# A recurrent layer and a mixture of experts in one kernel: a written order for the token sort, single fetches of the experts' rows, and small moves in the recurrent ticks

## The chip, the cores and the metric

The kernel runs on one core of a Trainium2 chip. A core has five engines that work beside each other and meet by semaphores: TensorE (PE in the profile; its weight loads are PEld), VectorE (DVE), ScalarE (ACT), GpSimd (POOL) and SyncE (SP), and 16 DMA engines. The metric is the device time of one launch in microseconds (us), as the median of several runs. Beside it stands one profiled execution, whose trace gives every instruction its start and duration.

## What is computed

The input is x, two sequences of 1024 tokens of 256 numbers, and one condition vector per sequence. Two layers are added to x, one after the other:

```python
# 1. two GRU layers over time, fed by a mixed input, with a gate from the condition
mixed = tanh(x @ W_in.T + b_in + cond)
h1 = gru(mixed, Wih0, Whh0, ...);  h2 = gru(h1, Wih1, Whh1, ...)
#   step: r = sigmoid(xr + hr); z = sigmoid(xz + hz); n = tanh(xn + r * hn)
#         h = (1 - z) * n + z * h
gate = sigmoid(cond @ W_gate.T + b_gate)
x = x + (gate * h2 + h2) @ W_out.T + b_out

# 2. a shared inner layer (512 wide) and 8 experts (256 wide), two experts a token
shared = (silu(xf @ w1) * (xf @ w3)) @ w2
s = sigmoid(concat(xf, cond) @ router_W);  top 2 of s + router_bias
gates = s[top] / sum(s[top])                      # 1/2 each where the sum is tiny
routed = sum over the two: gates * (gelu(xf @ W1e[e]) @ W2e[e])
x = x + (shared + routed) / 3
```

Everything is float32.

## The kernel before

**The ticks.** Each sequence is cut into 16 chunks, so that 32 chunks (the rows of a step) go through the recurrence at once. A first pass (`AHEAD`) gives each chunk a state to start from. The program is unrolled into 126 ticks; in one tick layer 0 makes a step and layer 1 makes the step that layer 0 had two ticks before. A step is `add_state` (the state times Whh, on TensorE, 16 matmul records) and `finish_scanned`: a sigmoid of two gates on ScalarE, a scan on VectorE, a tanh on ScalarE, a second product and a second scan on VectorE, and a transposition of the new row, which is the next step's weight operand. Each step waits for the one before, and both layers take turns on the same engines. Other work is hung into the ticks by name: `place(tick, where, what)` with `where` one of "product" (on TensorE, behind layer 0's products), "n0" (ScalarE), "scan0" and "scan1" (VectorE, between the tanh and the second scan of layer 0 or 1), "behind" and "end". `front.prepare` returns ten such small things that compute the condition's gate and the gated output weights. All of this stands in `tc.manual_schedule()`, in which each engine issues its instructions in the written order. At position -33 of a layer (ticks 29 and 31) the row that is the sequence's true beginning is set to zero by a mask (`keep_of`, `kept`); at position 0 (ticks 62 and 64) a layer starts its real pass from the state `begin`, whose turned form is `start_row`.

**The hidden parts.** The shared inner layer is computed in 16 parts, one for each block of 512 tokens (`TB`) and each 128 of the 512 inner columns. A part is a w1 sum and a w3 sum on TensorE (two matmuls each, of two records each), a sigmoid on ScalarE (`sig`), and two products on VectorE (`silu`, then the part itself, `front.hid`). Part 0 is computed in the last ticks; the other 15 are the list `parts`. The first `EARLY` of them run beside the sort, the next one behind the experts, and `parts[FILL:]` in the tail.

**The sort.** `moe` finds for each token its two experts, counts tokens by expert, gives each token's copy a slot so that blocks of 128 slots belong to one expert, and makes `pick` (which token sits in a slot) and `words` (which expert owns a block). That is a chain of some 50 VectorE instructions with two products on TensorE in it: a sum over all tokens (`ps_all`, `ps_before`), and `ps_pick`. The gates of the choice (`mine`, `denom`, `share`) follow it in the text. Here nothing fixes the order: the scheduler mixes the sort, the gates and the hidden parts on each engine.

**The experts.** `go_through` runs over 35 blocks of 128 slots (`SURE`), four more if a count asks for them (the branch). A block is fetched by an indirect DMA that GpSimd issues (`fetch`, L1274), turned on TensorE, multiplied with W1e, passed through gelu, turned, multiplied with W2e, and written to `back` in HBM.

**The tail.** A second written region. `fetch_back` issues an indirect DMA (L1335) that brings the experts' rows of 128 tokens for one of their two choices. Eight are issued at once. Then each part of `parts[FILL:]` is computed, and two more fetches are issued behind it: so that they don't run ahead, a one-element copy on GpSimd (the marker, L1334) reads one of the part's tiles and writes into the fetch's target. Only every second fetch has a marker. `add_gone` adds fetched rows, times their share, to `base` (L1349). Then 16 tiles follow: one more fetch, the product with w2 (`ps_s`, L1367, 8 records), an addition to `base` (L1375), and the output's DMA (L1376). All sums go through the seven PSUM banks of `p_any`, in turn.

Of the kernel before, what the change touches and what calls it, by code (L numbers as in the profile page):

```python
# [70 lines left out]
EARLY = 8  # L71
# [14 lines left out]
def gru_moe(ctx, tc, xT, vec, bias, w_in, wih0, whh0, wih1, whh1, w_out, w_gate, router, w1, w3, w2, w1e, w2e, out):  # L86
# [62 lines left out]
    class Steps:  # L149
# [177 lines left out]
        def finish_scanned(self, layer, to, tick, before_n, after_n, between, keep=None):  # L327
# [7 lines left out]
            if keep is not None:  # L335
                kept = self.edge.tile([P, U], FP, name=f"kept{layer}")
                nc.vector.tensor_scalar(kept, h, keep, -1.0, ALU.mult, ALU.mult)
                h = kept
# [14 lines left out]
            n = self.step_pool.tile([P, U, 2], FP, name=f"n{layer}")  # L353
            before_n()
# [46 lines left out]
    with ExitStack() as stack:  # L401
        g = Steps(stack, "", on_pe=False, rest_of_x=rest_of_x)
        g.gates = [
# [138 lines left out]

        def let_wait(ins, copied):


            if ins is not None and copied is not None:
                sync = mybir.DependencyInfo(mybir.DependencyClass.Sync, mybir.DependencyReason.DATA)
                tc.add_manual_dep(ins.ins, copied.ins.name, sync, reason="the next product adds to it")
# [48 lines left out]
        places = {}  # L597

        def place(tick, where, what):
            places.setdefault((tick, where), []).append(what)  # L600

# [49 lines left out]
        for i, todo in enumerate(front.prepare(g.bank)):  # L651
            for where, what in todo.items():
                place(AHEAD[0] - 8 + i, where, what)
# [32 lines left out]
        with tc.manual_schedule():  # L686
            for tick in range(AHEAD[0] + S + LAG):
                now = [layer for layer in range(2) if runs(layer, tick)]
                for layer in now:
                    if layer not in g.states:  # L690
                        g.states[layer], g.rows[layer] = zero_state, zero_row
                    elif position(layer, tick) == 0:
                        g.starts[layer] = g.states[layer] = begin[layer]
                        g.start_rows[layer] = g.rows[layer] = turned(g.starts[layer], f"start_row{layer}")
# [127 lines left out]
class Front:  # L822
# [17 lines left out]
    def prepare(self, bank):  # L840
# [3 lines left out]
        def gate_sums():  # L844
            ps["gate"] = bank("ps_gate")[:, 0 : KD * B].rearrange("p (k b) -> p k b", b=B)
            for m in range(KD):
                for k in range(KD):
                    last = nc.tensor.matmul(
                        out=ps["gate"][:, m, :],
                        lhsT=later["w_gate"][:, k, m * P : (m + 1) * P],  # L850
                        rhs=vec_sb[:, COND + k * B : COND + (k + 1) * B],
                        start=(k == 0),
                        stop=(k == KD - 1),
                    )
            return last
# [35 lines left out]
        def keep_context():  # L891
# [3 lines left out]
            {"product": gate_sums, "scan1": lambda: spread(0)},  # L895
            {"n0": gates, "scan1": lambda: spread(1)},
# [113 lines left out]
def moe(ctx, tc, tag, front, out):  # L1010
# [67 lines left out]
    def wide(t):  # L1078
        return t.to_broadcast([P, NT, E])

    iota = expert.unsqueeze(1).to_broadcast([P, NT, E])
    raw = rt("raw")
    nc.vector.tensor_tensor(raw, logits[:, :, 0:E], context.unsqueeze(1).to_broadcast([P, NT, E]), ALU.add)
    s = rt("s")
    nc.scalar.activation(s, raw, AF.Sigmoid)
    sel = rt("sel")
    nc.vector.tensor_tensor(sel, s, vec_sb[:, RBIAS : RBIAS + E].unsqueeze(1).to_broadcast([P, NT, E]), ALU.add)
    chosen = []
    for i in range(2):
        top = rt(f"top{i}", NT, 1)  # L1090
        nc.vector.tensor_reduce(top, sel, AX.X, ALU.max)
        at = rt(f"at{i}")
        nc.vector.tensor_tensor(at, sel, wide(top), ALU.is_equal)

        place = rt(f"place{i}")
        nc.vector.scalar_tensor_tensor(place, iota, float(E), at, ALU.subtract, ALU.mult)
        first = rt(f"first{i}", NT, 1)
        nc.vector.tensor_reduce(first, place, AX.X, ALU.min)
        nc.vector.tensor_scalar(first, first, float(E), None, ALU.add)
        one = rt(f"one{i}")  # L1100
        nc.vector.tensor_tensor(one, iota, wide(first), ALU.is_equal)
        chosen.append(one)
        if i == 0:
            rest = rt("rest")
            nc.vector.scalar_tensor_tensor(rest, one, -BIG, sel, ALU.mult, ALU.add)
            sel = rest
    both = rt("both", dtype=BF)
    nc.vector.tensor_tensor(both, chosen[0], chosen[1], ALU.add)


    for to, which in ((ps_all.rearrange("p (e t) -> p e t", e=E), every), (ps_before, before)):
        nc.tensor.matmul(out=to, lhsT=which, rhs=both.rearrange("p t e -> p e t"), start=True, stop=True)
    upto = rt("upto", E, NT)
    nc.vector.tensor_tensor_scan(
        upto.rearrange("p e t -> p (e t)"), running.rearrange("p e t -> p (e t)"), ps_all, 0.0, ALU.mult, ALU.add
    )

    whole = rt("whole", E, dtype=I32)
    nc.vector.tensor_scalar(whole, upto[:, :, NT - 1], float(P - 1), None, ALU.add)
    nc.vector.tensor_scalar(whole, whole, -P, None, ALU.bitwise_and)  # L1120
    size = rt("size", E)
    nc.vector.tensor_copy(size, whole)
    end = rt("end", E)
    nc.vector.tensor_tensor_scan(end, adding, size, 0.0, ALU.mult, ALU.add)
    slots_taken = rt("slots_taken", 1, dtype=I32)
    nc.vector.tensor_copy(slots_taken, end[:, E - 1 : E])
    start = rt("start", E)
    nc.vector.tensor_tensor(start, end, size, ALU.subtract)

    slot = rt("slot", E, NT)  # L1130
    nc.vector.tensor_tensor(slot, upto, ps_all.rearrange("p (e t) -> p e t", e=E), ALU.subtract)
    nc.vector.tensor_tensor(slot, slot, ps_before, ALU.add)
    nc.vector.tensor_tensor(slot, slot, start.unsqueeze(2).to_broadcast([P, E, NT]), ALU.add)
    slot_of = rt("slot_of", 2, NT)
    for c in range(2):
        own = rt(f"own{c}")
        nc.vector.tensor_tensor(own, chosen[c], slot.rearrange("p e t -> p t e"), ALU.mult)
        nc.vector.tensor_reduce(slot_of[:, c, :].unsqueeze(2), own, AX.X, ALU.add)
    slots = rt("slots", 2, NT, dtype=I32)
    nc.vector.tensor_copy(slots, slot_of)  # L1140
    block = rt("block", 2, NT, dtype=I32)
    nc.vector.tensor_scalar(block, slots, -P, None, ALU.bitwise_and)
    high = rt("high", 2, NT)
    nc.vector.tensor_copy(high, block)
    low = rt("low", 2, NT)
    nc.vector.tensor_tensor(low, slot_of, high, ALU.subtract)

    in_block = rt("in_block", 2, NT, NB, dtype=F16)
    at_lane = rt("at_lane", 2, NT, P, dtype=F16)
    for c in range(2):  # L1150
        nc.vector.tensor_tensor(
            in_block[:, c, :, :],
            block_start.unsqueeze(1).to_broadcast([P, NT, NB]),
            high[:, c, :].unsqueeze(2).to_broadcast([P, NT, NB]),
            ALU.is_equal,
        )
        nc.vector.tensor_tensor(
            in_block[:, c, :, :],
            in_block[:, c, :, :],
            token.unsqueeze(2).to_broadcast([P, NT, NB]),  # L1160
            ALU.mult,
        )
        nc.vector.tensor_tensor(
            at_lane[:, c, :, :],
            lane.unsqueeze(1).to_broadcast([P, NT, P]),
            low[:, c, :].unsqueeze(2).to_broadcast([P, NT, P]),
            ALU.is_equal,
        )
    for c in range(2):
        for t in range(NT):  # L1170
            nc.tensor.matmul(
                out=ps_pick,
                lhsT=at_lane[:, c, t, :],
                rhs=in_block[:, c, t, :],
                start=(c == 0 and t == 0),
                stop=(c == 1 and t == NT - 1),
            )
    pick = rt("pick", NB, dtype=I32)
    nc.vector.tensor_scalar(pick, ps_pick, float(N - 1), None, ALU.min)

    past = rt("past", NB, E)
    nc.vector.tensor_tensor(
        past,
        block_start.unsqueeze(2).to_broadcast([P, NB, E]),
        end.unsqueeze(1).to_broadcast([P, NB, E]),
        ALU.is_ge,
    )
    nc.vector.tensor_reduce(owner.rearrange("p w i -> p (w i)")[:, 0:NB].unsqueeze(2), past, AX.X, ALU.add)
    shifted = rt("shifted", NW, IDS)
    nc.vector.scalar_tensor_tensor(  # L1190
        shifted, owner, float(E - 1), power.unsqueeze(1).to_broadcast([P, NW, IDS]), ALU.min, ALU.mult
    )
    word = rt("word", NW, 1)
    nc.vector.tensor_reduce(word, shifted, AX.X, ALU.add)
    words = rt("words", NW, dtype=I32)
# [255 lines left out]
```

## Time and profile before

| | us |
|---|---|
| runs | 535.58, 538.12, 537.25 |
| median | 537.25 |
| the profiled execution | 538.56 |
| its span | 536.8 |
| busy in it: PE, PEld | 512.1, 341.2 |
| busy in it: DVE, ACT, POOL | 385.1, 243.6, 76.9 |

| stretch of the span | what runs |
|---|---|
| 0 to 10 | loads, first mixed input |
| 10 to 360 | the ticks |
| 360 to 389 | last group's output, the sort, hidden parts |
| 389 to 476 | the experts |
| 476 to 537 | the tail |

How to read it: times in the timeline are from the span's start; a row gives start, duration, engine, line, operation, output<-inputs and shapes, and in brackets how long the engine idled before and what ended that. A float32 matmul has two records. A matmul's start is recorded, its end is modelled.

### The profile page before, as it was taken

Reading aid. Unit: us, or ns where it says so; the run is one execution under the profiler, and the core shown is the slowest. Engines: PE = TensorE matmul, PEld = TensorE weight load, DVE = VectorE, ACT = ScalarE, POOL = GpSimd, SP = SyncE. Lnnn points to the kernel's source line nnn. Section 1 sums busy time; section 2 is a strip of 40 time slices with the busy share of each in tenths; the row PEclk is TensorE's granted clock in tenths of the full one; section 3 lists DMA queues with packets and bytes.
Section 4 is the critical chain, followed back from the end, with each engine's and each line's share of the span. In section 5 each row is a group of like instructions: output and inputs, shape, how many; then the busy total and the mean of one; then the engine's idle time right before and its main releaser. Section 6 shows DMA issues by size and latency. Waiting matters only on the chain. (4 is left out here: it accounts for less than half of the span.)

```text
span 536.8 us, 18511 instructions
## 1 busy us (share of the span) xinstructions
PE 512.1 (95%) x7492; PEld 341.2 (64%) x7492; DVE 385.1 (72%) x1296; ACT 243.6 (45%) x833; POOL 76.9 (14%) x124
## 2 busy tenths in 40 slices
PE   7999999999999999999999999989999999999795
PEld 4556766666665545665665666654458888854584
DVE  3665789999888888888888888888953333336372
ACT  3444355655665656656666565641133333341000
POOL 1200000000000000000000000002064444037570
PEclk9999999999999999999999999999999999999888
DMA  8980000000000000000000000001024443223252
GB/s 283 373 259 2 2 3 4 3 4 2 4 32 3 12 1 4 2 23 22 3 23 2 23 22 4 22 21 61 1 88 128 120 125 123 70 72 104 81 177 85
DMA packets 23103, 32.13 MB, mean 60 GB/s; under 512 B 3056, under 2 KB 18544, under 8 KB 22992
## 3 DMA queue, kind: packets, MB, share of 16 engines
q1 hardware_dynamic: 17344, 19.94, 11.0%
q0 software_dynamic: 3216, 8.79, 5.8%
q10 hardware_dynamic: 2448, 2.11, 1.2%
q8 instruction: 63, 1.03, 0.8%
q14 instruction: 32, 0.26, 0.2%
HBM read 21.26 MB, written 9.57 MB: 57 GB/s over the span
## 5 line engine op out<-in xcount | busy, mean ns | idle before, releaser
L296 PE MATMUL ps_step<-whh_sb,h 128*32 128x192 f32 x3616 | 193.3, 331 | 5.4 <-DVE h L369 4.2
L296 PEld LDWEIGHTS ps_step<-whh_sb,h 128*32 128x32 f32 x3616 | 94.6, 109 | 71.4 <-DVE h L369 51.9
L360 DVE TENSOR_TENSOR_SCAN row<-gates,n 128x128 f32<-128x128 f32 x230 | 98.0, 426 | 29.6 <-ACT n L355 28.3
L344 DVE TENSOR_TENSOR_SCAN ps_step<-gates,ps_step 128x128 f32<-128x128 f32 x230 | 97.3, 423 | 15.0 <-ACT gates L341 15.0
L268 PE MATMUL ps_step<-wih_sb,h 128*32 128x192 f32 x1696 | 99.7, 328 | 4.1 <-ACT ps_step L526 2.4
L355 ACT ACTIVATE n<-ps_step 128x64 f32<-128x64 f32 x228 | 53.0, 232 | 111.0 <-DVE ps_step L344 110.9
L341 ACT ACTIVATE gates<-ps_step 128x128 f32<-128x128 f32 x230 | 66.5, 289 | 35.5 <-PE ps_step L296 26.0
L268 PEld LDWEIGHTS ps_step<-wih_sb,h 128*32 128x32 f32 x1696 | 57.4, 110 | 26.8 <-ACT ps_step L526 14.5
L369 DVE STREAM_TRANSPOSE h<-row 128x64 f32<-128x64 f32 x230 | 56.5, 246 | 8.0
L969 PE MATMUL ps_w<-x_sb,w_sb 128*128 128x512 f32 x128 | 57.3, 597 | 0.2 <-PEq L1320 0.2
L268 PE MATMUL ps_in<-wih_sb,h 128*32 128x192 f32 x1024 | 54.4, 328 | 1.8 <-ACT h L257 1.4
L1239 DVE COPY hT<-ps_hT 128x256 f32<-128x256 f32 x35 | 14.9, 425 | 49.0 <-PE ps_hT L1237 47.1
L526 ACT COPY ps_step<-inputs 128x256 f32<-128x256 f32 x123 | 47.8, 389 | 0.0
L357 DVE SCALAR_TENSOR_TENSOR n<-gates,row 128x64 f32<-128x64 f32 x224 | 47.0, 210 | 0.0
L268 PEld LDWEIGHTS ps_in<-wih_sb,h 128*32 128x32 f32 x1024 | 34.0, 110 | 14.6 <-issue 4.6
L526 ACT COPY ps_step<-bt 128x256 f32<-128x256 f32 x106 | 39.9, 376 | 3.3
L1274 POOL DMA_INDIRECT inputs<-given,pick x35 | 33.3, 951 | 55.2 <-PE ps_xT L1237 31.9
L969 PEld LDWEIGHTS ps_w<-x_sb,w_sb 128*128 128x128 f32 x128 | 23.6, 190 | 27.1 <-issue 24.7
L1245 PE MATMUL ps_h<-w1e_sb,xT 128*128 x140 | 36.1, 380 | 0.7 <-DVE xT L1239 0.7
L1245 PE MATMUL ps_y<-w2e_sb,hT 128*128 x140 | 36.0, 380 | 0.0
L1335 POOL DMA_INDIRECT inputs<-back,slots x32 | 30.9, 964 | 30.0 <-issue 28.3
L1245 PEld LDWEIGHTS ps_y<-w2e_sb,hT 128*128 128x128 f32 x140 | 26.4, 190 | 4.8 <-DVE hT L1239 1.3
(179 smaller groups left out, 430.9 us busy)
## 6 DMA issues: line engine op xcount, KB each, us to landing
back<-y SPq DMA_DIRECT2D x35, 128.0 KB
w1e_sb<-in_w1e SPq DMA_DIRECT2D x1, 2048.0 KB
w2e_sb<-in_w2e SPq DMA_DIRECT2D x1, 2048.0 KB
given<-inputs SPq DMA_DIRECT2D x8, 256.0 KB
out_dram<-inputs ACTq DMA_DIRECT2D x16, 128.0 KB
whh_sb<-in_whh SPq DMA_DIRECT2D x2, 768.0 KB
x_sb<-in_xT SPq DMA_DIRECT2D x3, 512.0 KB
w_sb<-in_w SPq DMA_DIRECT2D x3, 512.0 KB
```

The source lines that it names most:

```text
L268: last = nc.tensor.matmul(out=out[cols(q), :, :], lhsT=given(k), rhs=self.wih[layer][:, k, q * 3 * U : (q + 1) * 3 * U].rearrange("p (g u) ...
L296: nc.tensor.matmul(out=by_sum(self.sums[layer])[cols(q), 0:3, :], lhsT=self.states[layer][:, k, :], rhs=self.whh[layer][:, k, q * 3 * U : ...
L341: nc.scalar.activation(gates[:, :, :, 1], sums[:, 1:3, :], AF.Sigmoid)
L344: nc.vector.tensor_tensor_scan(s, gates[:, 0, :, :].rearrange("p u i -> p (u i)"), ps[:, 0 : 6 * U : 3], 0.0, ALU.mult, ALU.add,)
L355: nc.scalar.activation(n[:, :, 0], s[:, 1 : 2 * U : 2], AF.Tanh, scale=-1.0 if keep is None else keep)
L357: nc.vector.scalar_tensor_tensor(n[:, :, 1], gates[:, 1, :, 1], 1.0, h, ALU.subtract, ALU.mult)
L360: nc.vector.tensor_tensor_scan(row.rearrange("p u i -> p (u i)"), gates[:, 1, :, :].rearrange("p u i -> p (u i)"), n.rearrange("p u i -> p ...
L369: nc.vector.transpose(to, row)
L526: return nc.scalar.copy(by_sum(banks[layer][tick % 2])[:, 0:4, :], g.sum_bias[1] if layer else inputs[:, group_of(0, tick), :, :],)
L969: last = self.tc.nc.tensor.matmul(out=ps, lhsT=self.later[name][:, k, m * P : (m + 1) * P], rhs=self.x1[:, k, blk * TB : (blk + 1) * TB], ...
L1245: nc.tensor.matmul(out=ps, lhsT=of[:, k, :], rhs=weights_sb[:, bass.ds(e * KD + k, 1), :], start=(k == 0), stop=(k == KD - 1),)
L1274: nc.gpsimd.indirect_dma_start(out=xg, out_offset=None, in_=given[:, :], in_offset=bass.IndirectOffsetOnAxis(ap=pick[:, i : i + 1], axis=0),)
```

## The change

- *Ticks.* The mask leaves `finish_scanned`; it is made by `mask(layer)`, placed one step earlier ("scan1" of tick 28 for layer 0, "scan0" of tick 31 for layer 1). The turned start row is made behind the first scan of its step and not ahead of the step. `gate_sums` is cut in two, one half a tick earlier, so `prepare` begins a tick earlier.
- *Sort.* It stands in a `manual_schedule` region, with six hidden parts at written places. In these parts ScalarE also copies the w3 sum out of PSUM (`look`), VectorE makes only the first product, and GpSimd makes the second (`silu_of`).
- *Gates last.* `mine` to `share` move from behind the sort to behind the experts, ahead of the branch.
- *`EARLY` is 7*, so one hidden part more (seven) lies in the tail.
- *Single fetches.* Each fetch in the tail whose caller gives a tile has a marker.

```diff
-EARLY = 8
+EARLY = 7
...
-            if keep is not None:
-                kept = self.edge.tile([P, U], FP, name=f"kept{layer}")
-                nc.vector.tensor_scalar(kept, h, keep, -1.0, ALU.mult, ALU.mult)
-                h = kept
...
+            if h is self.turned_row.get(layer):
+                nc.vector.transpose(h, self.states[layer])
             before_n()
...
+        def mask(layer):
+            kept = edge.tile([P, U], FP, name=f"kept{layer}")
+            nc.vector.tensor_scalar(kept, g.rows[layer], not_first[:, 0:1], -1.0, ALU.mult, ALU.mult)
+            g.rows[layer] = kept
+        place(AHEAD[0] - FIRST - 2, "scan1", lambda: mask(0))
+        place(AHEAD[0] + LAG - FIRST - 1, "scan0", lambda: mask(1))
...
-                place(AHEAD[0] - 8 + i, where, what)
+                place(AHEAD[0] - 9 + i, where, what)
...
-                        g.start_rows[layer] = g.rows[layer] = turned(g.starts[layer], f"start_row{layer}")
+                        g.start_rows[layer] = g.rows[layer] = g.turned_row[layer] = edge.tile(
+                            [P, U], FP, name=f"start_row{layer}"
+                        )
...
-            {"product": gate_sums, "scan1": lambda: spread(0)},
-            {"n0": gates, "scan1": lambda: spread(1)},
+            {"product": lambda: gate_sums(0), "scan1": lambda: spread(0)},
+            {"product": lambda: gate_sums(1), "scan1": lambda: spread(1)},
+            {"n0": gates},
...
+    def look(i):
+        factors[i] = [wk.tile([P, TB], FP, name=name) for name in ("sig", "silu", "other")]
+        nc.scalar.activation(factors[i][0], begun[i, "w1"], AF.Sigmoid)
+        nc.scalar.copy(factors[i][2], begun[i, "w3"])
+
+    def silu_of(i):
+        (blk, m), (sig, silu, other) = parts[i], factors[i]
+        nc.vector.tensor_tensor(silu, begun[i, "w1"], sig, ALU.mult)
+        nc.gpsimd.tensor_tensor(front.hid(m, slice(blk * TB, (blk + 1) * TB)), silu, other, ALU.mult)
+
+    with tc.manual_schedule():
+        sums_of(0)
...            # the sort, as before, with these calls in it:
+                look(0); sums_of(1); silu_of(0)          # behind the first choice's rest
...
+        look(1); sums_of(2)                              # behind the two counting matmuls
...
+        silu_of(1)                                       # behind slot
...
+        look(2); sums_of(3)                              # behind low
...                                                      # in_block[c], at_lane[c], then:
+            silu_of(2 + c)
+            if c == 0:
+                look(3); sums_of(4)
+        sums_of(5, ("w1",), [0])
...            # 32 matmuls for ps_pick, pick
+        look(4); silu_of(4); sums_of(5, ("w1",), [1]); sums_of(5, ("w3",))
...            # past, owner, shifted, word, words
+        look(5); silu_of(5)
+    shared_hidden(parts[6:EARLY])
...
     front.hidden(blk, m, *sums, *(wk.tile([P, TB], FP, name=name) for name in ("sig", "silu")))
+    mine = rt("mine", 2, NT)
...            # the gates' lines, moved here unchanged
...
-        if behind is not None and i % 2 == 0:
+        if behind is not None:
             nc.gpsimd.tensor_copy(yb[0:1, 0:1], behind[0:1, 0:1])
```

(Calls that stand on lines of their own in the kernel are joined by semicolons here.)

## The prediction

> **What bounds the kernel now.** I read the page's slices first, then the chain that ended last, then the timeline in three places: the ticks, the sorting (365 to 397 us) and the tail (476 us on). All times below are those of the one profiled execution (538.56 us; its span of 536.8 leaves 1.8 outside); the median of the runs is 537.25, so I take 1.3 off at the end.
>
> ```profile
> PE   7999999999999999999999999989999999999795
> PEclk9999999999999999999999999999999999999888
> ```
>
> TensorE is busy everywhere, but up to about 360 us that is a loop of short steps (a tick is 2.74 us, from one start of layer 0's gates to the next) in which TensorE, VectorE and ScalarE hand over to each other. From 365 us on it is plain TensorE work: whatever moves there moves the end only by TensorE's idle time and by its clock. The chain says the same of the tail, and shows a hole:
>
> ```profile
> 476.11 20.84 PE ps_w L969 x48
> 496.95 6.26 PE ps_s L1367 x29
> 503.21 0.46 issue
> ...
> 504.75 1.05 issue
> ...
> 506.26 1.65 issue
> 507.90 23.23 PE ps_s L1367 x94
> ```
>
> ```profile
> 496.00:503.00 7.00, 7.00 (x32) 5.65 (x31) 0.69 (x1) 0.60 (x1) 5.14 (x8) 1.00 0.33 94
> 503.00:508.00 5.00, 1.84 (x7) 1.28 (x7) 2.45 (x5) 0.00 (x0) 2.91 (x3) 0.87 0.37 107
> 508.00:513.50 5.50, 5.50 (x14) 4.12 (x14) 4.71 (x12) 0.00 (x0) 2.48 (x4) 0.50 0.28 91
> 513.50:531.20 17.70, 17.62 (x82) 15.18 (x80) 9.91 (x25) 0.00 (x0) 8.52 (x12) 1.00 0.53 160
> ```
>
> (The windows view: length, then busy time of PE, PEld, DVE, ACT and POOL; clock; DMA share; GB/s.) TensorE stops for 3.16 us between 503 and 508, and then runs at clock 0.50. The tail's price: 48 rows of w1/w3 at 0.43 and 128 rows of the w2 products at 0.216 (an undisturbed tile of 8 rows takes 1.73) are 20.6 + 27.6 = 48.2 us; from 476.11 to the last row's end at 531.1 it took 55.0. So 6.8 us are lost there. Just before, results of TensorE are taken late:
>
> ```profile
> 500.23 0.60 ACT L981 ACTIVATE sig<-ps_w 128x512 f32<-128x512 f32 x1 [6.71 <-PE ps_s L1367]
> 503.70 0.69 DVE L983 TENSOR_TENSOR inputs<-silu,ps_w 128x512 f32<-128x512 f32 x1 [2.15 <-remote]
> 508.65 0.42 DVE L1375 SCALAR_TENSOR_TENSOR inputs<-ps_s,inputs 128x256 f32<-128x256 f32 x1 [2.43 <-remote]
> ```
>
> The last inner part's w1 sum was due near 495.3, its sigmoid starts at 500.2; the first w2 tile was due near 498.7, its addition starts at 508.65. No row tells why; seven banks full of untaken sums fit TensorE's stop.
>
> The sorting's rows:
>
> ```profile
> 373.10 0.39 PE L1112 MATMUL few<-both,every 128*128 128x128 bf16 x1 [0.70 <-DVE both L1108]
> 388.06 0.19 DVE L1179 TENSOR_SCALAR pick<-few 128x39 int32<-128x39 f32 x1
> 388.55 1.18 POOL L1274 DMA_INDIRECT inputs<-given,pick  x1 [19.99 <-DVE pick L1179]
> 396.70 1.13 PE L1245 MATMUL ps_h<-w1e_sb,xT 128*128 x4 [0.68 <-DVE xT L1239]
> ```
>
> VectorE works without a break from 374 to 389, yet TensorE idles only 0.70 + 0.12 + 0.68 = 1.5 us here, for eight inner parts of 8 x 0.43 = 3.44 us fill it.
>
> **The change, part by part.** *The ticks.* Ticks 29, 31, 54 and 64 are 0.20, 0.19, 0.40 and 0.49 longer than 2.74.
>
> ```profile
> 92.12 0.21 DVE L337 TENSOR_SCALAR kept<-row,not_first 128x64 f32<-128x64 f32 x1
> 160.83 1.05 PE L848 MATMUL ps_gate<-vec_sb,w_gate_sb 128*128 128x2 f32 x8
> 189.77 0.24 DVE L484 STREAM_TRANSPOSE start_row<-begin 128x64 f32<-128x64 f32 x1
> ```
>
> The mask stands ahead of the scan that the tick waits for; moved one step up into the 0.18 us in which VectorE waits for the tanh, it saves about 0.1 each (the tanh with a scale tensor, 0.33 against 0.23, stays). Half of the gate sums, 0.53, fits a tick's slack, since ticks with a whole input piece (0.83) last 2.74 too: the 0.40 goes. The turned start row moves behind the scan, beside the tanh, and saves 0 to 0.2 (the rest of tick 64's excess is the go-round's copies, which stay). Sum -0.7 (-0.9 to -0.3, all on the path).
>
> *The sorting.* Out of VectorE's queue ahead of pick go some 2.5 us of gates, 1.5 us of block owners, and the second products (0.68 each); four first products (0.60 each in a row of independent steps) stay. But dependent steps follow each other at 0.32 where independent ones take 0.20, and the written order has nothing between them. Step by step: `both` at 371.4, earlier than TensorE ends its second part (365.27 + 2 x 3.44 = 372.15), so the two counting matmuls start there, not at 373.10, and the 0.70 hole closes. From the scan (372.85) to in_block took 5.7, now about 4.9: 377.75. Two rounds of 0.72 + 0.85 + 2.2 and one product of 0.6: 385.9. Pick at about 386.9, 1.2 us earlier than 388.06.
> TensorE meanwhile: 372.6 + three parts + a quarter part = 383.8, 16 pick matmuls (0.5), then nothing allowed until 386.0: **a hole of 1.6 us** (2.4 if GpSimd beside it slows VectorE by a tenth). Then 0.55 + 2.6 + 3.44: the filling ends at 392.6.
> The first fetch now stands behind GpSimd's products. A 128x512 product on GpSimd is not in the trace; bounds are VectorE's 0.69 and twice GpSimd's one-input row (128x512, 1.50), I take 1.5, being nearest that row in engine and size. Product 3 ends at 388.0, so fetch 0 starts no later than before; whether products 4 and 5 come between the fetches is the scheduler's. If not, TensorE's wait at the first expert stays 0.68; if both do, fetches 0 and 1 start near 391 and 393.5 and it is about 3.0. I take 1.7. Sum: 1.6 + 1.7 - 1.5 = **+1.8** (-0.8 if neither hole opens, +3.9 with both at their worst).
> [...]
> ScalarE's six copies (0.6 each, as its sigmoid of that size) hide: it is busy 15% of the time there. The gates' steps (2.5 us) move behind the experts, where VectorE is a third busy and the first share is wanted at 483.86; uncovered they would cost 2.5.
>
> *One part moved to the tail, single fetches.* The part's 3.44 us only changes place. GpSimd now issues a marker (0.18, with 0.27 behind it) before each of 23 fetches (11 before): 9 x 1.25 + 23 x 1.42 = 43.9 us, under a TensorE tail of 51.7; before it was 42.2 under 48.2. So fetches gain 1.6 us of room and cost nothing. Behind each marker wait all later fetches, and VectorE's first product of part k+2 now waits for the marker that reads part k's; by these periods the last starts at 500.4 on the old axis, with its bank wanted six tiles later. What the 6.8 us become is the open term: 0 to 6.8 back. I take 6.6, since all three late rows sit where the last part meets the w2 tiles, and that meeting is moved and re-spaced.
>
> **The rivals.** *A, the stop in the tail goes:* 538.56 - 0.7 + 1.8 - 6.6 = 533.1, less 1.3: **531.8** (529.5 to 535.5 with the terms' bounds). For it: the run of tiles after 513.5 keeps clock 1.00 with the same gathers and output writes. Against: its cause is not in the rows.
> *B, the stop stays:* what held TensorE's results was not the pairing of fetches. 538.56 - 0.7 + 1.8 - 1.3 = **538.4** (536 to 540.5). For it: fetches still follow each other within 1.4 us, and the runs of before lie within 2.5 us, so they all seem to pay.
> *C, slower: the stop stays and the hole ahead of pick halves the clock.* In the tail the clock went to 0.50 after 3.16 us of stops in about 5. The same 6.8 us at half clock cost 3.4: B + 3.4 = **541.8** (540 to 545). It decides once a hole, with what lies beside it, leaves TensorE idle for more than about 2 us of 3.4; at 360.10 an idle 1.29 us did not do it. My holes are 1.6 to 3.0.
> [...]
>
> **How the numbers follow.** A 0.43, B 0.30, C 0.27. A tenth of A falls within the 0.5% (2.7 us, about what measurement can tell from no change), a tenth of B beyond it as faster, a little as slower; C is nearly all slower. Faster 0.42, same 0.30, slower 0.28. The range runs from A's lower part to C's upper middle, 530 to 541.5; A alone is 529.5 to 535.5.
>
> **What would show it.** Right: no PE "issue" rows in the chain between parts and w2 tiles, and clock 1.00 to the end; ticks 29, 31, 54 near 2.8; pick near 387 on the old axis with PE idle about 1.6 ahead of it; DMA_INDIRECT for pick waiting on GpSimd's product, not on pick. Wrong: clock 0.50 in the sorting (C), a stop of 3 us again among the w2 tiles (B), or TensorE idle over 4 us ahead of the first expert.

## The result, and the profile after

The changed kernel takes **541.21 us** (median of seven runs, 540.17 to 543.61); the kernel before takes 537.59 on the same chip (seven runs, 535.58 to 538.83). The ratio is 1.0066, 95% interval 1.0042 to 1.0089: slower by 0.7%, where the likeliest case of the forecast (A, 531.8) was faster. The profiled execution took 540.17 us with a span of 538.4 (before: 538.56 and 536.8).

The page's slices after (TensorE's busy tenths and its granted clock):

```profile
PE   8999999999999999999999999989698999999995
PEclk9999999999999999999999999999999999999998
```

The dip in the tail at slice 38 is gone; the 6 at slice 29, at 377 to 390 us, is new. The chain that ended last (start, length, what):

```profile
479.27 24.27 PE ps_w L982 x56
503.54 8.52 PE ps_s L1421 x39
512.06 0.33 issue
...
513.49 0.33 issue
...
514.28 0.23 issue
514.51 18.30 PE ps_s L1421 x84
```

From the tail's start to the last w2 row it is 53.5 us for 51.7 of work, with three short stops and at full clock. Before it was 55.0 for 48.2. So the tail lost 1.8 us instead of 6.8: **5.0 less**. The windows of the sorting (length; busy time of PE, PEld, DVE, ACT and POOL; clock; DMA share; GB/s) show where more than that went:

```profile
384.60:388.90 4.30, 0.04 (x2) 0.03 (x2) 4.26 (x4) 0.80 (x2) 1.33 (x1) 1.00 0.01 2
388.90:392.40 3.50, 3.50 (x20) 1.95 (x21) 3.24 (x6) 0.60 (x1) 2.63 (x3) 0.51 0.02 5
```

TensorE stands still for 4.3 us while VectorE is busy throughout, and then runs 3.4 us at half clock. The timeline tells what VectorE did until then:

```profile
369.16 0.28 DVE L1355 TENSOR_TENSOR score<-one,s 128x128 f32<-128x128 f32 x1
369.20 1.37 POOL L1122 TENSOR_TENSOR h<-silu,other 128x512 f32<-128x512 f32 x1 [1.44 <-DVE silu L1121]
369.36 1.36 DVE L1138 TENSOR_TENSOR at<-rest,top 128x128 f32<-128x128 f32 x1
...
373.95 0.41 DVE L1164 TENSOR_TENSOR_SCAN upto<-running,few 128x128 f32<-128x128 f32 x1
...
377.04 1.29 POOL L1122 TENSOR_TENSOR inputs<-silu,other 128x512 f32<-128x512 f32 x1 [6.47 <-issue]
377.42 1.13 DVE L1188 TENSOR_TENSOR own<-one,slot 128x128 f32<-128x128 f32 x1
380.51 0.81 DVE L1210 TENSOR_TENSOR in_block<-in_block,token 128x624 f16<-128x624 f16 x1
...
384.62 1.33 POOL L1122 TENSOR_TENSOR inputs<-silu,other 128x512 f32<-128x512 f32 x1 [6.30 <-DVE silu L1121]
384.87 1.75 DVE L1210 TENSOR_TENSOR in_block<-in_block,token 128x624 f16<-128x624 f16 x1
388.88 0.70 PE L1229 MATMUL few<-in_block,at_lane 128*128 128x39 f16 x16 [4.26 <-DVE at_lane L1216]
...
389.61 0.20 DVE L1237 TENSOR_SCALAR pick<-few 128x39 int32<-128x39 f32 x1 [0.19 <-PE few L1229]
391.00 1.22 POOL L1306 DMA_INDIRECT inputs<-given,pick  x1 [0.17 <-issue]
```

Two things are to be seen. Four VectorE steps with two SBUF inputs (`at`, `own`, `in_block`, `past`) start while a GpSimd product runs, and each ends 0.15 to 0.67 us behind that product: `at` takes 1.36 us, `in_block` 1.75 where the same step, alone, takes 0.81. `score`, which starts 0.04 us ahead of a product, keeps its 0.28; `shifted`, which starts at 391.71 during a fetch's issue and 0.55 us ahead of a product, takes 1.88 (0.20 in v_products). And the gates are not last: `score` (L1355) stands at 369.16; eleven of the gates' small steps come ahead of the scan `upto`, which the rest of the sort waits for.

From the first filling part (365.27 before, 364.47 after) to pick it is 22.8 us before and **25.1** after. From the first filling part to the tail it is 110.84 before and 114.80 after, with one part of 3.44 less in it: 7.4 us more. Of these 1.55 are one wait at 406 us for a late result, of the kind that the tail of before had, and 5.9 are the sort's:

```profile
407.63 1.13 PE L1277 MATMUL ps_y<-w2e_sb,hT 128*128 x4 [1.55 <-DVE hT L1271]
```

To within 0.1 us the 5.9 are made up of TensorE's idle time, 5.8 us (0.83 + 4.26 + 0.68) where before has 1.5 (0.70 + 0.12 + 0.68), and of half the 3.41 us at half clock, 1.7. The sort starts 0.8 earlier than before; with that and the tail's -5.0 it is the +1.6 of the spans.

### The profile page after: what moved, and what is told of

Its sections match the earlier page's. It is cut to its first block, busy times and chain, and to the rows that moved or that the text cites. A ratio compares the mean times of both kernels' runs of the same rounds, so it can differ in the third digit from the quotient of the medians.

```text
span 538.4 us, 18557 instructions
## 1 busy us (share of the span) xinstructions
PE 511.7 (95%) x7492; PEld 340.4 (63%) x7492; DVE 388.7 (72%) x1290; ACT 247.3 (46%) x839; POOL 88.9 (17%) x142
## 3 DMA queue, kind: packets, MB, share of 16 engines
q8 instruction: 63, 1.03, 0.8%
## 5 line engine op out<-in xcount | busy, mean ns | idle before, releaser
L353 ACT ACTIVATE n<-ps_step 128x64 f32<-128x64 f32 x228 | 53.1, 233 | 110.7 <-DVE ps_step L340 110.7
L982 PE MATMUL ps_w<-x_sb,w_sb 128*128 128x512 f32 x128 | 58.5, 608 | 0.1
```

What stands on the lines that cost most here:

```text
L353: nc.scalar.activation(n[:, :, 0], s[:, 1 : 2 * U : 2], AF.Tanh, scale=-1.0 if keep is None else keep)
L982: last = self.tc.nc.tensor.matmul(out=ps, lhsT=self.later[name][:, k, m * P : (m + 1) * P], rhs=self.x1[:, k, blk * TB : (blk + 1) * TB], ...
```

## The experiments

Four groups of kernels ran on four chips, each beside the kernel before on its chip. Pick is counted from the first filling part; two expectations (gates_last, late_products) count it from a row 2.0 us earlier, so that their 27.2 is 25.1 here. "Hole" is TensorE's idle time ahead of pick's second products, "stretch" runs from the first filling part to the tail, "tail" to the last w2 row, "idle" is how much longer than its rows at full clock (48.2 us with six parts, 51.7 with seven) the tail was; 0.2 to 0.3 there is no stop, since a row of w1 or w3 takes 0.434 us and not 0.43. In no_products and best the tail is counted from the start of a wait ahead of it.

| kernel | before there | median | ratio (95%) | pick | hole | clock 0.50 for | stretch | tail, idle |
|---|---|---|---|---|---|---|---|---|
| before (shown) | 537.59 | | | 22.8 | 0 | 6.83 in the tail | 110.8 | 55.0, 6.8 |
| after (shown) | 537.59 | 541.21 | 1.0066 (1.0042, 1.0089) | 25.1 | 4.26 | 3.41 | 114.8 | 53.5, 1.8 |
| v_products | 531.25 | 536.11 | 1.0095 (1.0067, 1.0123) | 24.8 | 3.50 | 3.41 | 112.0 | 51.9, 0.2 |
| no_products | 531.25 | 536.33 | 1.0100 (1.0083, 1.0117) | 22.2 | 2.47 | 0 | 108.5 | 53.3, 1.6 |
| old_sort | 531.25 | 531.82 | 1.0016 (1.0006, 1.0025) | 22.8 | 0 | 0 | 108.2 | 51.9, 0.2 |
| single | 531.25 | 534.50 | 1.0060 (1.0043, 1.0077) | 22.8 | 0 | 0 | 110.6 | 48.5, 0.3 |
| before_again | 531.38 | 531.46 (one run) | | 22.8 | 0 | 0 | 110.6 | 48.5, 0.3 |
| after_again | 531.38 | 537.18 | 1.0103 (1.0086, 1.0120) | 25.1 | 4.25 | 6.83 | 114.2 | 51.9, 0.2 |
| gates_last | 531.38 | 537.53 | 1.0106 (1.0085, 1.0128) | 24.0 | 3.47 | 3.41 | 112.1 | 52.9, 1.2 |
| late_products | 531.38 | 533.53 | 1.0047 (1.0033, 1.0061) | 21.5 | 1.77 | 0 | 108.5 | 52.9, 1.2 |
| ticks_only | 531.98 | 531.03 | 0.9985 (0.9977, 0.9994) | 22.8 | 0 | 0 | 110.6 | 48.5, 0.3 |
| pairs | 531.98 | 537.00 | 1.0101 (1.0087, 1.0116) | 25.1 | 4.27 | 3.41 | 112.7 | 51.9, 0.2 |
| fill | 531.98 | 536.46 | 1.0084 (1.0069, 1.0098) | 25.0 | 1.69 | 6.83, later | 114.0 | 51.9, 0.2 |
| best | 531.98 | 534.45 | 1.0050 (1.0038, 1.0063) | 22.2 | 0 | 0 | 110.7 | 49.9, 1.7 |
| before_c | 536.79 | 539.05 (one run) | | 22.8 | 0 | 6.83 in the tail | 110.9 | 55.8, 7.6 |
| after_c | 536.79 | 540.53 | 1.0072 (1.0046, 1.0098) | 25.1 | 4.26 | 6.83 | 114.2 | 53.9, 2.2 |
| early7 | 536.79 | 537.13 | 1.0016 (1.0000, 1.0031) | 22.8 | 0 | 0 | 110.6 | 53.8, 2.1 |
| pairs_c | 536.79 | 541.37 | 1.0076 (1.0042, 1.0111) | 25.1 | 4.26 | 3.41 | 114.8 | 53.3, 1.6 |

### The sorting: whose are the 7.4 us?

**v_products**, the second products on VectorE:

```diff
-        nc.gpsimd.tensor_tensor(front.hid(...), silu, other, ALU.mult)
+        nc.vector.tensor_tensor(front.hid(...), silu, other, ALU.mult)
```

> The changed kernel with the six second products of the sorting (silu x other, 128x512) on VectorE instead of GpSimd; everything else as changed. Theory 1 (contention): VectorE's steps with two SBUF inputs wait for GpSimd's product beside them, so at, own, in_block and shifted go back from 1.36, 1.13, 1.75 and 1.88 us to about 0.28, 0.29, 0.80 and 0.20; four products of 0.6 to 0.7 come into VectorE's queue ahead of pick, so pick stays within 0.5 of where it is (25.14 after the first filling part), the hole ahead of it stays near 4, but fetch 0 follows pick at 0.5 instead of 1.4 and the stretch up to the tail is 1 to 3 us shorter: 538 to 540 in all. Theory 2 (the written order with its dependent spacing is what is slow, GpSimd takes no part): the four rows stay stretched, pick comes 2.7 later, hole near 7: about 544.

The timeline of v_products, the same steps:

```profile
370.39 0.29 DVE L1138 TENSOR_TENSOR at<-rest,top 128x128 f32<-128x128 f32 x1
...
377.46 0.36 DVE L1188 TENSOR_TENSOR own<-one,slot 128x128 f32<-128x128 f32 x1
...
384.94 0.81 DVE L1210 TENSOR_TENSOR in_block<-in_block,token 128x624 f16<-128x624 f16 x1
388.00 0.71 PE L1229 MATMUL few<-in_block,at_lane 128*128 128x39 f16 x16 [3.50 <-DVE at_lane L1216]
```

All are back at 0.29, 0.36 and 0.81, in the same written order, so it is GpSimd that stretched them, and theory 1 holds. Pick moved by 0.35 only, because four products of 0.6 to 0.7 came into VectorE's queue ahead of it; the ratio is 1.0095 where the changed kernel unchanged has 1.0103 (after_again). So the edit's main idea gains nothing: the second products cost VectorE about as much time on GpSimd as on VectorE itself (2.9 and 2.6 us ahead of pick, against no_products below).

**no_products**, the second products left out:

```diff
-        nc.gpsimd.tensor_tensor(front.hid(...), silu, other, ALU.mult)
+        nc.scalar.copy(front.hid(...), silu)
```

> The changed kernel with the six second products of the sorting left out: ScalarE copies silu to their place (128x512, about 0.6 each, ScalarE is idle most of that time), so neither GpSimd nor VectorE has them. It prices what GpSimd's products do to the rest. Theory 1 (contention): at, own, in_block, past and shifted go back to 0.28, 0.29, 0.80, 0.48, 0.20, pick comes about 2.8 earlier (near 22.3 after the first filling part), the 4.26 us hole shrinks to about 1.5 and TensorE keeps clock 1.00: about 4 to 6 us less than the changed kernel, 535 to 537. Theory 2 (order, not GpSimd): pick at most 0.5 earlier, the hole stays near 4, clock 0.50 stays: 539.5 to 541.

Its rows ahead of pick:

```profile
383.18 0.81 DVE L1210 TENSOR_TENSOR in_block<-in_block,token 128x624 f16<-128x624 f16 x1
386.25 0.58 PE L1229 MATMUL few<-in_block,at_lane 128*128 128x39 f16 x16 [2.47 <-DVE at_lane L1216]
386.87 0.20 DVE L1237 TENSOR_SCALAR pick<-few 128x39 int32<-128x39 f32 x1
```

Pick came 2.9 us earlier than in the changed kernel (expected 2.8), the clock stayed at 1.00, and the stretch is 4.2 shorter than that of pairs, which has the changed sort and 3.41 us at half clock. The rows are theory 1's. The total is not: 1.0100 against 1.0103, some 1 us instead of 4 to 6, for 1.4 us went to a wait of TensorE for VectorE's queue at the branch ahead of the tail, and 1.8 came behind the last w2 row. The causes of both are open.

**gates_last**: the gates' first writes read the last hidden part, so that the scheduler cannot take them forward.

```diff
+        nc.vector.tensor_copy(score[:, 0, 0:1], front.hid(m, slice(blk * TB, blk * TB + 1)))
         nc.vector.tensor_tensor(score, chosen[c], s, ALU.mult)
```

> The changed kernel with the gates' 14 small steps really last (their first writes are tied to the last inner part's product behind the experts, so that they cannot be taken forward into the sorting); the same work plus two copies of one column. Theory 1 (contention is the larger part): pick 1.0 to 1.6 us earlier, at 25.6 to 26.2 after the first filling part instead of 27.2, the hole ahead of it about 3, the clock may still go to 0.50: 1 to 3 us less than the changed kernel. Rival (the gates that were taken forward are the whole of the lateness): pick at 24.5 or earlier, hole under 2, 5 us less.

Pick is 1.1 us earlier, as theory 1 had it; the hole is still 3.47 and the clock still falls. The time did not improve (537.53 against 537.18 on the same chip, 1 to 3 less expected): against pairs, which has as much half clock, the stretch is 0.6 shorter, and the tail took 1.0 back, since the gates now lie where it starts. "Gates last" in the changed kernel's text had no such tie, and outside of a written region the scheduler took them forward into the sort.

**late_products**: gates tied as above, and the second products on VectorE behind pick; the w3 sums wait in rows of the fetches back.

```diff
+        other = rows[:, AWAY + 2 * i : AWAY + 2 * i + 2, :]...   # parts 0 to 3
-        nc.gpsimd.tensor_tensor(front.hid(...), silu, other, ALU.mult)
...
         silu_of(5)
+        for i in range(6):
+            second_product(i)
```

> The changed kernel with the gates really last and the second products on VectorE behind pick (ScalarE keeps the w3 sums in the rows that the fetches back use later), so GpSimd and VectorE share nothing in the sorting and pick waits for four first products alone. Theory 1: pick near 23 after the first filling part (24.25 without products, less 1.0 to 1.6 for the gates), hole 1 to 1.5, clock 1.00, stretch up to the tail 107 to 108.5 instead of 114.8: 6 to 8 us less than the changed kernel, within 1 us of before. Theory 2 (the written order is slow in itself): pick later than 24.8, hole above 2.5: less than 4 us gained.

Pick at 21.5, 3.6 earlier than in the changed kernel, hole 1.77, clock 1.00, stretch 108.5. Against the changed kernel on the same chip 3.65 us are gained, not 6 to 8: 1.21 are waited at the first expert, and the tail is 1.0 longer for the gates at its start. The written order, once rid of both faults, is 1.3 us earlier at pick than the scheduler's, but the kernel still is slower than before: TensorE idles 1.77 and 1.21 us in the stretch, where before idles 1.5 in all, and the tail is longer.

**fill**: the same work, the whole sixth part ahead of pick's products.

```diff
-        sums_of(5, ("w1",), [0])
+        sums_of(5)
         for c in range(2): ...            # pick's products
-        sums_of(5, ("w1",), [1]); sums_of(5, ("w3",))
```

> The changed kernel with the whole sixth filling part ahead of pick's products on TensorE instead of a quarter of it (the same work in another order). The hole ahead of pick goes from 4.25 to about 1.65, the 2.6 us are then missing behind pick and TensorE waits 2 to 3 at the first expert. Theory: the length of one hole sets the clock, both holes stay under 3.4, clock 1.00 throughout, and the 1.7 to 3.4 us of half clock are gained: 534 to 535.5. Rival: the clock goes by the sum of the idle time, and falls to 0.50 all the same: 536.5 to 538.

The time hardly moved (536.46 against pairs' 537.00 on the same chip), as the rival had it. The hole shrank to 1.69 as expected, but the clock fell all the same, behind another stop of 1.95 us at the first turned row (windows of fill):

```profile
386.75:388.45 1.70, 0.01 (x2) 0.01 (x1) 1.70 (x2) 0.00 (x0) 0.00 (x0) 1.00 0.00 0
388.45:392.50 4.05, 4.05 (x24) 1.82 (x24) 3.85 (x9) 2.65 (x4) 2.90 (x3) 1.00 0.00 0
392.50:394.60 2.10, 0.15 (x2) 0.14 (x2) 0.25 (x2) 0.32 (x1) 1.91 (x3) 1.00 0.48 125
394.60:401.40 6.80, 6.10 (x19) 4.50 (x19) 2.64 (x6) 0.77 (x2) 5.71 (x6) 0.50 0.23 67
```

My theory that one hole must be as long as 3.4 us (holes of 3.47 to 4.26 had halved the clock in four kernels, 2.47 and 1.77 in two others had not) fell with it. What the runs show instead is told in the last section.

### The tail: is the stop the kernel's?

**before_again** and **after_again** are the two kernels unchanged.

> The kernel before, unchanged, for a profile on the chip of these experiments. The comparison runs of before gave 531.25 on the chip of the first four experiments, against 537.25 in the shown runs. Theory a: the stop among the w2 tiles and the half clock behind it (6.8 us) are not the kernel's own but come and go between chips: here the tail lasts about 48.5 us from 476 on, without a stop, clock 1.00. Theory b: the difference lies elsewhere (shorter ticks, other ending): tail 55 as shown, the rest 6 us shorter.

> The changed kernel, unchanged, beside before_again. If the tail's stop is absent from before on this chip, the change has nothing to take back there: the sorting's +7.4, the ticks' -0.8 and nothing from the tail: 5 to 7 us slower than before. If the stop is there, 3 to 4 us slower, as in the shown runs.

The chain of before_again has no stop at all:

```profile
475.77 20.84 PE ps_w L969 x48
496.61 27.64 PE ps_s L1367 x128
```

Theory a holds: on three of four chips the kernel before takes 531.3 to 532.0 and loses nothing in its tail. There the change has nothing to take back, and it is slower by 1.03% (5.8 us).

**old_sort** is the changed kernel with the sorting and the gates of before:

```diff
-    with tc.manual_schedule():
-        sums_of(0) ...                    # the written sort
+    iota = ...                            # the sort and the gates as before
+    shared_hidden(parts[:EARLY])
```

> The changed kernel with the sorting and the gates of the kernel before (ticks, seven filling parts and single fetches as changed). If the 7.4 us more up to the tail all belong to the sorting's rewriting and the tail's 5 us less do not: the stretch up to the tail goes back to 110.84 - 3.44 = 107.4, the tail stays near 53.5 with clock 1.00, and the whole is 531 to 534, faster than both. If the tail's stop depends on the state in which the sorting leaves the experts (rival): a stop of about 3 us among the w2 tiles and clock 0.50 come back, 536 to 539.

5.4 us are gained on the changed kernel's 537.2 on another chip without the stop, so nearly all of the loss is the sorting's. It is not faster than before: with seven parts instead of eight less work lies behind pick, and TensorE waits 1.28 there instead of 0.68.

**single** is before with a marker ahead of every fetch:

```diff
-        if behind is not None and i % 2 == 0:
+        if behind is not None:
```

> The kernel before with single fetches alone (a marker ahead of every fetch back). If the pairing of the fetches caused the stop among the w2 tiles: the tail goes from 55.0 to 50 or less and the whole to 531 to 533.5. If not (the number of parts in the tail, or their distance from the w2 tiles, decides): stop and clock 0.50 stay, 536 to 539.

Neither case: 3.25 us slower. TensorE's tail is as short as in before_again, but the chain that ended last now runs over GpSimd's queue (chain of single):

```profile
518.78 0.98 POOL inputs L1335
...
520.21 4.33 DMA inputs<-back,slots
524.65 0.49 DVE inputs L1349
```

This gather is issued at 520.21 and lands only when TensorE is through (524.5); one more is issued at 521.65 and lands at 525.0. From the first fetch (477.60) to there, 23 markers and 32 fetches take 47.4 us, as long as a tail of six parts. **pairs**, the changed kernel with paired fetches, shows that with seven parts this room is there:

```diff
-        if behind is not None:
+        if behind is not None and i % 2 == 0:
```

> The changed kernel with the fetches back in pairs again (a marker ahead of every second one). Where the tail has no stop, TensorE is busy from its start to the last w2 tile in either form, so the time is that of the changed kernel within 0.5 us, about 537. Rival: the 12 markers more cost GpSimd's queue time that the end waits for, as in the kernel before with single fetches (+3.1 us): then 2 to 3 us less, 534 to 535.

537.00 against 537.18 on another chip without the stop: no difference, as expected.

The last four kernels ran on a chip that has the stop. The profiled run of before_c (539.05) lies above all other runs of before there (534.49 to 538.94), so its losses are at the high end.

> The kernel before, unchanged, on another chip. If the stop of the shown runs belongs to some chips only, most likely none here: tail 48.5 us from its first part, 531 to 532 in all. If it is there: 536 to 538, with late updates of TensorE near 495 to 509.

> The changed kernel, unchanged, beside before_c. Without the stop 5 to 6.5 us slower than before (about 537); with it 3 to 4 us slower.

> The kernel before with seven filling parts instead of eight, nothing else. Without the stop: the part's 3.44 us move to the tail, TensorE waits 0.3 to 1.3 more at the first expert because less work lies behind pick: 0.3 to 1.3 us more than before. With the stop, if the extra part in the tail is what avoids it: 4 us less than before.

> The changed kernel with paired fetches. Without the stop as the changed kernel within 0.7 us. With the stop, if single fetches are what avoids it: 4 to 6 us more than the changed kernel.

The timeline of before_c, ScalarE's sigmoids of the parts, and its chain:

```profile
489.90 0.60 ACT L981 ACTIVATE sig<-ps_w 128x512 f32<-128x512 f32 x1 [2.09 <-PE ps_w L969]
492.59 0.60 ACT L981 ACTIVATE sig<-ps_w 128x512 f32<-128x512 f32 x1 [2.09 <-POOL inputs L1334]
499.44 0.60 ACT L981 ACTIVATE sig<-ps_w 128x512 f32<-128x512 f32 x1 [6.25 <-PE ps_s L1367]
```

```profile
505.03 2.15 issue
507.19 0.59 PE ps_s L1367
507.77 0.84 issue
508.61 22.96 PE ps_s L1367 x94
```

The sigmoid that is due at 495.3 starts at 499.44, nearly as in the shown run (500.23); in before_again it starts at 495.30. early7 has the late sigmoid too:

```profile
491.96 0.60 ACT L981 ACTIVATE sig<-ps_w 128x512 f32<-128x512 f32 x1 [2.08 <-DVE inputs L1349]
500.87 0.60 ACT L981 ACTIVATE sig<-ps_w 128x512 f32<-128x512 f32 x1 [8.31 <-PE ps_w L969]
```

So have after_c (504.56) and pairs_c (506.95). TensorE's results come late from some 494 to 502 us on in every kernel on this chip, whatever part it is at; but with seven parts in the tail TensorE's stops (over 0.25 us each) add up to 0.7 to 1.1 us there and the clock stays, and in the two profiles with six they add up to 3.2 and 3.9 us and halve it. Pairs or single fetches make no difference to that (pairs_c 1.6, after_c 2.2 idle). Why the seventh part would shelter TensorE is not shown. By the medians it is worth less than by the profiles: from the chips without the stop to the one with it, before lost 5.4 us (531.4 to 536.8) and the changed kernel 3.35 (537.18 to 540.53), so the change takes back 2 us in the median. early7, which has the seventh part and nothing else, was expected 4 us ahead of before if the part avoids the stop; it came out 0.3 behind (1.0016), with 1.83 us of waiting for a late result at 401 us in its profile. pairs_c is 0.8 us slower than after_c in the median, not the 4 to 6 that would make the single fetches the cause.

### The ticks, and an attempt to beat both

**ticks_only** is before with the masks, the halved gate sums and the start row of the change, and nothing else.

> The kernel before with the ticks' edits alone (masks beside the tanh, gate sums in two halves, the start row behind the scan); sorting, eight filling parts and paired fetches as before. The sorting starts 0.6 to 0.8 us earlier and everything behind it moves with it: 0.6 to 0.8 less than before, ratio near 0.9987. Rival: the time saved in the ticks is waited for later (at pick or the experts): ratio 1.000.

0.95 us less, ratio 0.9985 (0.9977 to 0.9994, which is 0.3 to 1.2 us): the only part of the change that pays by itself, and the fastest kernel of the study. The profiles put the gain at about half of that (see the account below). **best** adds the repaired sort: late_products' sort, the whole sixth part ahead of pick's products as in fill, the gates tied to the eleventh block, eight filling parts, paired fetches.

> An attempt to beat both: the ticks' edits; the written order with the second products on VectorE behind pick, the gates tied to the eleventh expert block, the whole sixth part ahead of pick's products, eight filling parts and paired fetches. Pick near 23.5 after the first filling part, no hole ahead of it, 0.7 or less at the first expert: 1.0 to 1.6 us less than before, 529.8 to 530.6. Rival: the six second products delay the first turned rows on VectorE, TensorE waits 1 to 2 us at the first expert: 531 to 532.

The rival came true. There is no hole ahead of pick, but the six second products stand ahead of the first turned row's copy on VectorE, and TensorE waits for that (timeline of best):

```profile
396.40 1.13 PE L1283 MATMUL ps_h<-w1e_sb,xT 128*128 x4 [2.15 <-DVE xT L1277]
...
476.89 3.67 PE L982 MATMUL ps_w<-x_sb,w_sb 128*128 128x512 f32 x8 [1.43 <-DVEq L1388]
```

The second row is the wait at the branch again, 1.43 us. With both the stretch is where before has it (110.7 against 110.6), the tail 1.4 longer, and the kernel 0.5% slower.

## Why the prediction was wrong

- **The ticks: right within their bounds.** -0.7 was taken (-0.9 to -0.3), and ticks_only is 0.95 faster. The sort starts 0.80 earlier in the shown pair, but 0.43 of that is there already at the 25th sigmoid of the ticks (72.19 us against 72.62), ahead of every edit. From there to the first filling part the five profiles without the edits take 292.6 to 292.7 us and the thirteen with them 292.0 to 292.3: 0.5 less on average. Of the single terms, the halved gate sums gave the 0.4 taken (55.5 us from the 61st sigmoid to the 101st, now 55.0 to 55.1), and the first mask 0.1; the second mask gave almost nothing, and from the 101st to the 116th sigmoid, around the start row, it is 0.1 longer and not shorter (21.3, now 21.4 to 21.5).
- **The sorting: the step that failed.** The prediction took +1.8, 3.9 at the worst, and 7.4 came (5.9 without the late result). The sum's pick at 386.9 is 21.6 us behind the first filling part; 25.1 was measured. Two terms of that step were wrong. GpSimd's product was priced by its own length (1.5 taken, 1.26 to 1.37 measured, well hit) and what it does to VectorE at nothing but "a tenth" in the worst case, a term that no run shows; in its place the runs show 2.9 us ahead of pick (no_products). And 2.5 us of gates were taken out of VectorE's queue on the text's word; they stayed in, which costs 1.1 (gates_last). With both repaired, late_products has its pick at 21.5 and its hole at 1.77 (1.6 taken): the rest of the working holds to 0.2 us.
- **What the product does to VectorE stands in no row of before.** Before has no product of two inputs on GpSimd. With the change, `at` (0.28 in before, with no GpSimd step beside it) ends 0.15 us behind the product, at 370.72 against 370.57.
- **The hole and the clock.** 1.6 us was taken, 4.26 came. The bound from which the clock falls, "about 2 us of 3.4", an estimate, fits the runs (TensorE idled 1.87 of the 3.41 us ahead of before's halving at 506.66, and 1.94 and 1.95 in gates_last and fill), but the sum used it in rival C alone, together with a stop that stays. What came is A's tail, in the main, with C's sorting, a case that had no chance of its own: the two conditions of C are independent, and each should have had its own chance. The half clock cost 1.7 us here, not C's 3.4.
- **The first expert.** 1.7 us of waiting was taken, 0.68 came, though fetch 0 stood behind a product until 391.00 as foreseen: pick itself was 3.5 us late and the half clock cost 1.7, so TensorE still had filling parts to do.
- **The tail.** -6.6 was taken for the shown chip, -5.0 came in the profiled pair, some -2 in the medians. The mechanism was open in the prediction, and it was a wrong guess that the meeting of parts and tiles makes the late results: they come with the chip (or its session, since each chip had one), and are absent on three others. All runs at hand came from one chip, so that their agreement proved nothing about the kernel. That C's 541.8 lies close to the measured 541.21 is luck: C has 5.2 for the sorting and nothing back from the tail, where 7.4 and -5.0 came in the profiled pair.
- **Single fetches cost nothing:** right beside seven parts (pairs), and only there; alone they cost 3.25 us (single). The sum counted the fetches' issues and left out the time to landing, 4.33 us in the chain of single. By its own periods (21 x 1.25 + 11 x 1.42) it also has 41.9 and not 42.2 us for before; nothing hangs on that.

## What to carry to other kernels

Work that was moved to an idle engine had a price here on the engine that it was moved away from (pick came 2.9 us later for it): look at which of that engine's steps will lie beside it, and count a VectorE step with two SBUF inputs that starts beside a GpSimd product as waiting for the product's end (four such steps ended 0.15 to 0.67 us behind it). A stage whose bound engine idles 1.5 us of 111 can win no more than that from a new order, and can lose much more; price the edit against that first. And where text is moved to make something late, look for what keeps the scheduler from taking it forward again: here only a data dependence did.

## What the runs showed of the hardware

- **The clock changed at whole multiples of 3.41 us, and was halved behind as little as 1.87 us of idle time in 3.41.** In both shown traces a whole number of 3.413 us lies between two changes of the clock (before: 6.83 is two, 20.48 six; the 382.29 ahead of the changed kernel's halving are 112, the 143.36 behind its half clock 42), and in the experiments the half clock of the table lasted 3.41 or 6.83. Laying a grid of 3.41 us from each change of the clock, the window ahead of a halving held 1.87 (before, shown), 1.94 (gates_last), 1.95 (fill), 2.37 (before_c) and 3.27 to 3.41 us (the changed kernels) of TensorE idle time. Without effect stayed 1.85 (best), 1.83 (early7) and 1.71 (pairs_c) and, at the kernels' ends, 1.88 (no_products) and 1.91 (before_again). So about 1.9 of 3.41 decides in these runs, no sharper than that since the ends of matmuls are modelled, and a hole of 2.47 us did nothing where the grid cut it into 1.19 and 1.28 (no_products). The half clock lasted one window where the next one held 0.46 us of idle time or less, and two where it held 0.70 to 1.25.
- **TensorE's results came late on one chip and not on others.** In the shown run of before the semaphore updates that tell of sums done at 496.95 and 498.67 us came at 503.68 and 508.62, and those of four tiles within 0.28 us, while the matmul rows ran on at full rate (four tiles from 496.79 on at 1.73 us each, TensorE's first stop at 503.21). The shown runs' chip and the fourth of the experiments (whether they are the same is not recorded) had it in six profiles, from some 495 us on, and in three of these once more near 400 us (1.55 to 1.83 us of waiting); the other three chips had it in none of twelve. It is worth 5.4 us of the kernel before in the medians. Whether the chip or the time of its session makes it is not told apart, and its cause stays open.
